# Two halves of a weight load either side of a clearing write: the opening of a mixture-of-experts kernel on one core

## The chip, the cores and the metric

The kernel runs on one core of a Trainium2 chip. The metric is the device time of one execution in microseconds (us), as the median of several runs. The core has five engines that run beside each other and wait for each other through semaphores: TensorE (PE: matmuls, with weight loads shown as PEld), VectorE (DVE), ScalarE (ACT), GpSimd (POOL) and SyncE (SP, which here only issues DMAs). Sixteen DMA engines serve all queues of the core: q1 is SyncE's, q10 ScalarE's, q0 GpSimd's (the indirect transfers).

## What is computed

The input x has 16 x 256 tokens of 128 numbers. Three layers follow each other, each on a layer-normed x: a mixture of experts, an attention without softmax over the keys, and the same mixture of experts again.

```python
x = x + 0.5 * ffn(layernorm(x), norm_scale, gate_w, gate_b, w1, b1, w2, b2)
x = x + attn(layernorm(x), Wq, bq, Wk, bk, Wv, bv, Wfq, bfq, Wfk, bfk)
x = x + 0.5 * ffn(layernorm(x), norm_scale, gate_w, gate_b, w1, b1, w2, b2)

# ffn, for T tokens, 32 experts, 4 chosen per token
t = rmsnorm(x) * norm_scale
vals, idx = top_k(t @ gate_w.T + gate_b, 4)
combine = zeros(T, 32) with softmax(vals) at idx
h1 = einsum('th,efh->tef', t, w1) + b1
glu, lin = min(h1[..., ::2], 7), clip(h1[..., 1::2], -7, 7)
h = glu * sigmoid(1.702 * glu) * (lin + 1) * combine[:, :, None]
out = x + einsum('tef,ehf->th', h, w2) + combine @ b2
```

Only the four chosen experts of a token have a weight, so the kernel computes these alone: it sorts the tokens by expert, and runs every expert on its own rows.

## The kernel before

**Tiling.** The 4096 tokens are two groups of four blocks of 512 tokens (four tiles of 128). The sorted rows of a group lie in DRAM in xs[g], and the experts' results in ys[g]; a row holds five tokens of one expert, and one expert step takes four times 25 rows (125 tokens each).

**Preparation (L129 to L270).** SyncE issues, in this order: small constants, the four x blocks of group 0 (L136), b1 (L138), w1 in four loads of 1024 KB, eight experts each (L244 to L246), the clearing of xs[0] in 14 writes of 500 KB from a zero tile (L252 to L255), w2 in four loads (L257 to L259), and zeros for the tail of ys (L266). The clearing is needed because experts read whole rows of xs and the sort fills only some of them; what it writes is overwritten where the sort has something to put. Group 1 has no such clearing: its dispatch is called with clear=True and scatters zeros to the free rows only.

**Folding w1.** `folded` (L293) multiplies a weight by the matrix `less`, which takes the mean over the input dimension off and scales by norm_scale; one TensorE product for two experts (two matmuls of 512 columns each in the trace), one ScalarE copy back into w_sb (L299). `fold_experts(c)` (L303) does experts 2c and 2c+1, so 16 folds cover w1; folds 0 to 3 need w1's first load, 4 to 7 the second, 8 to 11 the third, 12 to 15 the fourth. The PSUM tag "ph" that they write has two buffers.

**Routes and dispatch.** `routes` (L957) is a generator: norm coefficients of four blocks, then for each block the gate, the four best experts, their weights and ranks (`route`, L437 to L515), with a yield between pieces. `dispatch` (L519 to L668) is the sort of a group: its first piece counts rows per expert for the whole group (L524 to L570), the second makes the expert tables (pex, L577), and then for each of the four blocks one piece makes the row numbers (L628 to L645) and four pieces, one a tile, gather tokens with one-hot matmuls (p_f, L665), copy them to one of three buffers s (L669, L670) and scatter them to xs by an indirect DMA on GpSimd's queue (L589). So a group has 16 scatters. Each of them must follow the clearing of xs[0].

**Order of the work.** Generators wait in a queue; `step(n)` runs n pieces, `finish()` the rest. For group 0 the program appends routes(0), and writes 16 times step(2) and a fold; then the load of b1's rows into the last row of w_sb (L1015, which must follow all folds, since they read that row), finish, two constants (minus, mask), dispatch of group 0 and finish, `fold_attention` (L307), and the experts of group 0 with group 1's routes beside them. `experts` (L684) loads xq from xs on SyncE's queue (L696), copies the step's weights from w_sb on GpSimd (L703), transposes (L709), multiplies (L723, L741) and writes ys (L748). This written order isn't the order on the engines: the builder places each instruction on its engine's queue by its written place and by when it takes it to be ready, and each engine then runs its queue in that order.

Of the kernel before, what the change touches and what calls it, by code (L numbers as in the profile page):

```python
# [22 lines left out]
P = 128  # L23
# [5 lines left out]
NE = 32  # L29
# [27 lines left out]
def kernel(  # L57
# [22 lines left out]
    nc = tc.nc  # L80
# [160 lines left out]


    w_sb = wpool.tile([P, NE, EW], F32, tag="w_sb", name="w_sb")
    for c in range(NE // 8):  # L244
        s = slice(c * 8, (c + 1) * 8)
        nc.sync.dma_start(w_sb[:, s, 0 : 2 * P], w1[:, s].rearrange("h e t f -> h e (t f)"))  # L246
    FILLS = NT // NJ // 2
    part = NB * BW // P // (2 * FILLS)
    rows = xs[0][0:NB, :].rearrange("n w -> (n w)").rearrange(
# [2 lines left out]
    for i in range(FILLS):  # L252
        nc.sync.dma_start(
            rows[:, i],
            zero.rearrange("p r h -> p (r h)")[:, 0:part].unsqueeze(1).to_broadcast([P, 2, part]),  # L255
        )
    for c in range(NE // 8):  # L257
        s = slice(c * 8, (c + 1) * 8)
        nc.sync.dma_start(w_sb[:, s, 2 * P : EW], w2[:, s])  # L259
# [31 lines left out]
    LAST = P - 1  # L291

    def folded(w, name, out=None):  # L293

        pw = ps_h.tile([P, TB], F32, tag="ph", name=f"pw_{name}")[:, 0 : math.prod(w.shape[1:])]
        nc.tensor.matmul(pw, less, w, start=True, stop=True)
        if len(w.shape) > 2:
            pw = pw.rearrange("p (e c) -> p e c", e=w.shape[1])
        nc.scalar.copy((w if out is None else out)[0:LAST], pw[0:LAST])  # L299
# [3 lines left out]
    def fold_experts(c):  # L303

        folded(w_sb[:, 2 * c : 2 * c + 2, 0 : 2 * P], f"w{c}")
# [620 lines left out]
    def step(n=1):  # L926
        for _ in range(n):
            while waiting:
                try:
                    next(waiting[0])  # L930
                    break
                except StopIteration:
                    waiting.popleft()

    def finish():
        while waiting:
            step()
# [19 lines left out]
    def routes(g, gap, most):  # L957
        srcs = []
        for b in range(GB):
            if g > 0:  # L960
                load_x(g * GB + b)
            srcs.append(x_tiles.pop(g * GB + b))
        co = coefficients(srcs, f"f{g}")
        yield

        def block(b):
            yield from route(first[g], srcs[b], b, co[:, :, b * NJ : (b + 1) * NJ])

        yield from staggered((block(b) for b in range(GB)), gap, most)
# [38 lines left out]
    b1_rows = dram.tile([NE, 2 * P], F32, tag="b1_rows", name="b1_rows")  # L1008
    nc.scalar.dma_start(b1_rows, b1_t)

    waiting.append(routes(0, 1, GB))
    for c in range(NE // 2):
        step(2)
        fold_experts(c)
    nc.sync.dma_start(  # L1015
        w_sb[LAST:P, :, 0 : 2 * P], b1_rows.rearrange("(o e) c -> o e c", o=1)
    )
    finish()

    minus = const.tile([P, NJ, P], BF16, tag="minus", name="minus")  # L1020
# [16 lines left out]


    waiting.append(dispatch(first[0]))
    finish()  # L1040
    banks.clear()
    banks.append((ps_bg, "bg"))
# [72 lines left out]
```

## Time and profile before

| | us |
|---|---|
| median of 3 runs (lowest to highest) | 747.09 (746.89 to 747.17) |
| the profiled execution | 768.92 |
| its span | 767.2 |
| PE busy in the span | 646.2 (84%) |
| DVE, ACT, POOL busy | 489.8, 385.8, 291.2 |
| granted TensorE clock, mean | 0.922 |

The profile is one execution, recorded with the profiler on, and longer than the runs. A row of a timeline gives the start in us from the span's start, the duration, the engine and line, the operation with what it writes and reads, and in brackets how long the engine was idle before and what ended that (inferred from semaphores). Some rows of the opening, which the change touches:

```profile
7.71 6.38 SPq L246 DMA_DIRECT2D w_sb<-in_w_dram  x4
14.20 27.58 SPq L253 DMA_DIRECT2D xs<-zero  x14
42.78 6.76 SPq L259 DMA_DIRECT2D w_sb<-in_w_dram  x4
52.66 1.36 SPq L1015 DMA_DIRECT2D w_sb<-b_rows  x1
```

These are times of issue on SyncE's queue, not of landing; a group of issues is merged into a row with their number.

### The profile page before, as it was taken

To read this page: it belongs to the slowest core of one execution; us is meant where nothing else is said; L and a number is where in the kernel's file an instruction comes from. 1 tells how busy PE (TensorE), PEld (TensorE's weight loads), DVE (VectorE), ACT (ScalarE), POOL (GpSimd) and SP (SyncE) were. 2 spreads that over 40 slices of the span, in tenths; PEclk is the share of its full clock that TensorE was granted. 3 is DMA by queue.
4 is the path that set the end of the run, shared out by engine and by line. 5 is a ranking of instruction groups with operands and counts; after the bars stand their busy time and mean duration, and the time that the engine had idled before them with its cause. 6 is when DMAs were issued, how large, how long until landed. Compare 5 with 4: busy or idle time off the path is not lost. (4 is left out here: it accounts for less than half of the span.)

```text
span 767.2 us, 16355 instructions
## 1 busy us (share of the span) xinstructions
PE 646.2 (84%) x4995; PEld 602.6 (79%) x5009; DVE 489.8 (64%) x1833; ACT 385.8 (50%) x918; POOL 291.2 (38%) x583
## 2 busy tenths in 40 slices
PE   3877598879969998897987889888889769999776
PEld 1567588879868888896886889878878659999776
DVE  6864777755527988965763587678767436654534
ACT  2843498445517458465452547464665414545410
POOL 3024433676363432121464231321226265543152
PEclk9978799999979999997998988898989979999989
DMA  7997355665565635223446342522435466766464
GB/s 235 369 334 280 124 148 163 216 234 188 144 165 137 175 84 149 55 83 108 168 168 187 112 144 69 139 79 68 107 111 184 155 157 196 222 170 176 118 185 157
DMA packets 136924, 123.98 MB, mean 162 GB/s; under 512 B 9858, under 2 KB 123970, under 8 KB 136834
## 3 DMA queue, kind: packets, MB, share of 16 engines
q1 hardware_dynamic: 121890, 73.16, 33.8%
q0 software_dynamic: 10960, 44.90, 17.5%
q10 hardware_dynamic: 3984, 4.82, 1.8%
q8 instruction: 45, 0.74, 0.4%
q14 instruction: 45, 0.37, 0.1%
HBM read 58.80 MB, written 64.04 MB: 160 GB/s over the span
## 5 line engine op out<-in xcount | busy, mean ns | idle before, releaser
L703 POOL COPY w_l<-w_sb 128x256 f32 x192 | 72.5, 407 | 144.5 <-PE ph_l L723 124.4
L703 POOL COPY w_f<-w_sb 128x256 f32 x192 | 74.0, 417 | 121.7 <-PE ph_f L723 108.3
L723 PE MATMUL ph_f<-xT_f,w_f 128*128 128x125 f32 x768 | 104.7, 285 | 2.9 <-DVE lin_f L728 1.6
L723 PE MATMUL ph_l<-xT_l,w_l 128*128 128x125 f32 x768 | 102.5, 284 | 0.0
L723 PEld LDWEIGHTS ph_f<-xT_f,w_f 128*128 128x128 f32 x768 | 98.0, 201 | 4.8 <-POOL w_f L703 2.7
L723 PEld LDWEIGHTS ph_l<-xT_l,w_l 128*128 128x128 f32 x768 | 96.6, 200 | 1.0 <-issue 0.9
L728 DVE TENSOR_SCALAR lin_f<-ph_f 128x250 f32<-128x250 f32 x96 | 39.3, 413 | 56.5 <-ACT a_f L727 46.5
L728 DVE TENSOR_SCALAR lin_l<-ph_l 128x250 f32<-128x250 f32 x96 | 39.4, 413 | 56.1 <-ACT a_l L727 55.5
L665 PE MATMUL p_f<-tn_f,o_f 128*128 128x128 f32 x320 | 47.1, 310 | 14.6 <-ACT s_f L669 6.5
L665 PEld LDWEIGHTS p_f<-tn_f,o_f 128*128 128x128 f32 x320 | 44.3, 221 | 16.9 <-ACT s_f L669 7.2
L741 PE MATMUL po_l<-w_sb,a_l 128*125 x384 | 55.3, 288 | 2.5 <-DVE a_l L733 1.7
L741 PE MATMUL po_f<-w_sb,a_f 128*125 x384 | 53.9, 283 | 3.1 <-ACT yq_f L746 1.3
L741 PEld LDWEIGHTS po_l<-w_sb,a_l 128*125 128x125 f32 x384 | 49.8, 200 | 4.2 <-ACT yq_l L746 2.1
L727 ACT ACTIVATE a_f<-ph_f 128x250 f32<-128x250 f32 x96 | 36.3, 384 | 33.3 <-PE ph_f L723 23.2
L727 ACT ACTIVATE a_l<-ph_l 128x250 f32<-128x250 f32 x96 | 36.0, 380 | 33.7 <-PE ph_l L723 27.1
L814 PE MATMUL pu_f<-gt_f,u_f 128*128 128x128 f32 x320 | 48.5, 295 | 5.0 <-DMA gt_f<-ys,row_f 4.5
L814 PE MATMUL pu_l<-gt_l,u_l 128*128 128x128 f32 x320 | 44.0, 283 | 9.0 <-DMA gt_l<-ys,row_l 7.7
L741 PEld LDWEIGHTS po_f<-w_sb,a_f 128*125 128x125 f32 x384 | 47.9, 194 | 4.6 <-ACT yq_f L746 2.6
L814 PEld LDWEIGHTS pu_l<-gt_l,u_l 128*128 128x128 f32 x320 | 40.8, 197 | 12.1 <-issue 8.5
L784 POOL DMA_INDIRECT gt_f<-ys,row_f x32 | 32.3, 1010 | 47.1 <-PE pu_f L814 25.6
L814 PEld LDWEIGHTS pu_f<-gt_f,u_f 128*128 128x128 f32 x320 | 43.8, 208 | 6.2 <-DMA gt_f<-ys,row_f 3.5
L589 POOL DMA_INDIRECT xs<-s_f,row_f x32 | 31.1, 972 | 44.7 <-ACT s_f L670 21.6
(338 smaller groups left out, 1464.0 us busy)
## 6 DMA issues: line engine op xcount, KB each, us to landing
xq_f<-xs SPq DMA_DIRECT2D x48, 224.0 KB
ys<-yq_f SPq DMA_DIRECT2D x48, 224.0 KB
xq_l<-xs SPq DMA_DIRECT2D x48, 224.0 KB
ys<-yq_l SPq DMA_DIRECT2D x48, 224.0 KB
xs<-zero SPq DMA_DIRECT2D x14, 500.0 KB
w_sb<-in_w_dram SPq DMA_DIRECT2D x4, 1024.0 KB
x<-in_x_dram SPq DMA_DIRECT2D x8, 256.0 KB
xr_f<-xr_f ACTq DMA_DIRECT2D x8, 256.0 KB
```

The costliest lines, as they stand in the source:

```text
L589: ins = nc.gpsimd.indirect_dma_start(out=xs[st.g][:, :], out_offset=bass.IndirectOffsetOnAxis(ap=index, axis=0), in_=rows.rearrange("p r h ...
L665: nc.tensor.matmul(p0[:, r, :] if r < 4 else p1[:, 0:P], o[:, r, :], k.tn[:, t, :], start=True, stop=True,)
L703: nc.gpsimd.tensor_copy(w[:, s, :], w_flat[:, bass.ds(at[2 * c + s], 2 * P)])
L723: nc.tensor.matmul(ph[:, part, s, 0:RT], w_q[c][:, s, part * P : (part + 1) * P], x_q[:, 2 * c + s, :], start=True, stop=True,)
L727: nc.scalar.activation(a[:, ts, :], ph[:, 0, :, 0:RT], AF.Silu, scale=ALPHA)
L728: nc.vector.tensor_scalar(lin[:, ts, :], ph[:, 1, :, 0:RT], LIMIT + 1.0, 1.0 - LIMIT, ALU.min, ALU.max,)
L741: nc.tensor.matmul(po[:RT, t, :], hT[:, t, :], w_flat[:, bass.ds(at[t] + 2 * P, P)], start=True, stop=True,)
L784: nc.gpsimd.indirect_dma_start(out=gt.rearrange("p r h -> p (r h)"), out_offset=None, in_=ys[st.g][:, :], in_offset=bass.IndirectOffsetOnA ...
L814: nc.tensor.matmul(pu[:, t, :], u[:, r, s, :], got[t][:, r, :], start=(r == 0), stop=False)
```

## The change

The load of w1 becomes a function, and half of its loads (EARLY = 2 of four) stay ahead of the clearing of xs[0]; the other two go behind the clearing and ahead of w2. Folds 0 to 7 are written between three pieces of the routes each, and the routes are finished behind them. The constants minus and mask follow as before. Then the dispatch of group 0 is appended, and folds 8 to 15 are written after one piece of it each; b1's rows are loaded after fold 15, and the rest of the dispatch follows. No instruction is added or left out.

```diff
-    for c in range(NE // 8):
-        s = slice(c * 8, (c + 1) * 8)
-        nc.sync.dma_start(w_sb[:, s, 0 : 2 * P], w1[:, s].rearrange("h e t f -> h e (t f)"))
+    def load_w1(lo, hi):
+        for c in range(lo, hi):
+            s = slice(c * 8, (c + 1) * 8)
+            nc.sync.dma_start(w_sb[:, s, 0 : 2 * P], w1[:, s].rearrange("h e t f -> h e (t f)"))
+
+    EARLY = 2
+    load_w1(0, EARLY)
...
+    load_w1(EARLY, NE // 8)
     for c in range(NE // 8):
         s = slice(c * 8, (c + 1) * 8)
         nc.sync.dma_start(w_sb[:, s, 2 * P : EW], w2[:, s])
...
     waiting.append(routes(0, 1, GB))
-    for c in range(NE // 2):
-        step(2)
+    for c in range(4 * EARLY):
+        step(3)
         fold_experts(c)
-    nc.sync.dma_start(
-        w_sb[LAST:P, :, 0 : 2 * P], b1_rows.rearrange("(o e) c -> o e c", o=1)
-    )
     finish()
...
     waiting.append(dispatch(first[0]))
+    for c in range(4 * EARLY, NE // 2):
+        step()
+        fold_experts(c)
+    nc.sync.dma_start(
+        w_sb[LAST:P, :, 0 : 2 * P], b1_rows.rearrange("(o e) c -> o e c", o=1)
+    )
     finish()
```

## The prediction

> **What bounds the kernel now.** I read the page's slices first, then the stage that the change touches: the DMA queues by stretch, GpSimd's and ScalarE's timelines, and the waits of SyncE's queue. Of the page:
>
> ```profile
> PEclk9978799999979999997998988898989979999989
> DMA  7997355665565635223446342522435466766464
> ```
>
> Each column is 19.2 us. The DMA engines are full only in the first three columns; after that TensorE carries the time (busy 84% of the span). So the first 84 us are a stage of their own with another limit, and what ends it is in SyncE's waits of the first 150 us and in TensorE's row after it:
>
> ```profile
> SPq L696 <- DMA xs<-s_f,row_f: 25.1, 1, 25.1
> 87.19 1.06 PE L709 MATMUL pxT_f<-ident,xq_f 125*128 125x125 f32 x4 [7.91 <-DMA xq_f<-xs]
> ```
>
> The experts' first load waits for the last of the first group's 16 scatters, and TensorE has nothing before it lands. The time that counts is the issue of scatter 16; a shift of it moves the next 680 us with it. GpSimd's timeline of the 16 issues (cut):
>
> ```profile
> 49.68 1.15 POOL L589 DMA_INDIRECT xs<-s_f,row_f  x1 [14.71 <-DMA w_sb<-in_w_dram]
> 51.13 0.97 POOL L589 DMA_INDIRECT xs<-s_f,row_f  x1 [0.30 <-issue]
> 52.41 0.96 POOL L589 DMA_INDIRECT xs<-s_f,row_f  x1 [0.30 <-issue]
> 56.84 0.97 POOL L589 DMA_INDIRECT xs<-s_f,row_f  x1 [3.35 <-ACT s_f L670]
> ...
> 66.61 0.96 POOL L589 DMA_INDIRECT xs<-s_f,row_f  x1 [3.88 <-ACT s_f L670]
> ...
> 81.44 0.96 POOL L589 DMA_INDIRECT xs<-s_f,row_f  x1 [1.34 <-DVE st_f L344]
> ```
>
> Two paces: from issue 1 (49.68) to issue 7 (66.61) six intervals of 2.82 us; from there to issue 16 (81.44) nine of 1.65 us. Why the first is slow is in ScalarE's timeline and in the DMA queues, for 49.7 to 66 and then for 66 to 84 us:
>
> ```profile
> 46.79 0.27 ACT L670 COPY s_f<-p_f 128x128 f32<-128x128 f32 x1
> 55.81 0.59 ACT L669 COPY s_f<-p_f 128x512 f32<-128x512 f32 x1 [4.43 <-DMA xs<-s_f,row_f]
> ```
> ```profile
> DMA packets 4522, 5.77 MB, mean 354 GB/s; under 512 B 207, under 2 KB 4191, under 8 KB 4521
> q1 hardware_dynamic: 4121, 4.07, 80.6%
> q0 software_dynamic: 400, 1.69, 26.0%
> ```
> ```profile
> DMA packets 958, 3.65 MB, mean 203 GB/s; under 512 B 196, under 2 KB 262, under 8 KB 956
> q0 software_dynamic: 880, 3.55, 50.0%
> q1 hardware_dynamic: 76, 0.07, 1.1%
> ```
>
> s_f has three buffers, so the fourth copy waits until scatter 1, issued at 49.68, has landed at 55.81: 6.1 us, beside SyncE's backlog (q1: w2, ys zeros, group 1's x). After 66 us the backlog is gone and copies, TensorE and GpSimd set the pace. The first issue has another gate: its rows were ready at 46.79 + 0.27 = 47.06 us, GpSimd issued at 49.68. The row names w_sb, a load that a scatter doesn't need; of what it does need the DMA queue's last is the clearing of xs, 14 x 500 KB behind all of w1. I take the clearing as the gate (the releaser is inferred); q1's packets turn from 2 KB to 512 B (w2) between 45 and 47 us, which fits.
>
> **The change, part by part.**
>
> *The order on SyncE's queue.* Nothing is added or removed; two of the four 1024 KB loads of w1 (2.10 MB) go behind the clearing. From 16 to 44 us all queues together moved 10.30 MB (368 GB/s), 9.17 MB of it on q1, 328 GB/s. So the clearing ends between 2.10 / 0.368 = 5.7 and 2.10 / 0.328 = 6.4 us earlier; I take 5.8: the gate opens at 43.9. The late half of w1 lands where the clearing ended, its first piece at about 43 to 46 us. Moved behind it, w2, ys zeros, b1_rows and x of group 1 keep their place in bytes. b1_rows now waits for fold 15 in the sort and x of group 1 is queued behind it, but x landed near 66 us and its first user (bn_stats) runs at 77.5: some 10 us of cover, and without it about as much as the slip beyond.
>
> *Folds 8 to 15.* Eight times two matmuls (1.02 us a fold at full clock, 1.7 at half) and one ScalarE copy of 0.59 us leave the routes and go beside the first sort: 8.2 us of TensorE, 4.7 us of ScalarE. In the routes VectorE is busy 11.07 of 12.50 us (24 to 36.5), so they end at most 1 to 2 us sooner. From 36.5 to 44.2 ScalarE is busy 7.33 of 7.70; three fold copies (1.75 us) vanish from there. The first rows are then ready at about 47.06 - 1.5 - 1.75 = 43.8, level with the new gate. In the new place, 49.7 to 66, TensorE is busy 10.1 and ScalarE 3.5 of 16.3 us: the folds fit; I charge 0.3 us. Without that cover, or queued ahead of the sort, see the third rival.
>
> *step(3) and step(1), dispatch, minus and mask appended elsewhere.* Order only, no instruction more; mask and minus already run at 12.6 us. At nothing, plus or minus 1 us for a different order later on.
>
> *What an earlier first scatter is worth.* Not its 5.8 us, as the bytes are the same. Each scatter (5.24 MB / 16 = 0.328 MB) that moves before the backlog's end puts that end off by 0.328 / 0.354 = 0.93 us, and saves 1.65 us afterwards. With k more of them: k = (5.8 + 0.93 k) / 2.82, so k = 3.1; gain 3.1 x (1.65 - 0.93) = 2.2 us. Less 0.3 for the folds: **1.9 us**.
>
> [...] The row has 6.1 us for the first, 2.82 us between issues, and q0 26% of the engines. I go by the row.
>
> The profiled execution takes 768.92 us (span 767.2, 1.7 around it), the median of the runs 747.09; the 22 us between lie all over the execution. The shift is early and absolute, so it carries over one to one: 768.92 - 1.9 = 767.0 profiled, 747.1 - 1.9 = **745.2**. A measurement here tells about 0.2% (1.5 us) from no change.
>
> **The rivals.**
>
> *The start passes wholly (10%).* [...]
>
> *The start doesn't move (18%).* GpSimd's row names w_sb, and the rows were ready only at 47.06. If sort or another load sets issue 1, it stays within 1 to 2 us of 49.68 and k is below 1: 747.
>
> *Slower: TensorE stands at a fold (24%).* TensorE takes matmuls in order. Of the first sort, past's product, the row numbers and the first rows follow dispatch's first step, and folds 8, 9, 10 are written between these. If they are also issued so, the first rows stand behind w1's third piece, here about 45 us: then three folds at the half clock of that stretch (PEclk 0.50, 44.2 to 49.7), 5.1 us, ten matmuls of the first tile 2.1 us, copies and issue 1.0 us: issue 1 at 53.2, 3.5 us late. k = -3.5 / (2.82 - 0.93) = -1.9, x 0.72 = 1.3 us lost; the same wait for the fourth piece beside scatters adds 0 to 2, I take 0.6. 747.1 + 1.3 + 0.6 = 749. It decides when fold 8 stands ahead of the first tile's matmuls and its piece lands after 43 us. For it: order as written, and folds did wait for w_sb before (2.3 us in two waits). Against: in the profile instructions aren't in written order, fold_attention's matmuls (L315) run at 40.37 ahead of dispatch's L650, so the builder takes what it believes ready.
>
> **How the numbers follow.** Main case 48%, 743 to 746.8 (start 2 to 6 us earlier, order plus or minus 1). With the rivals: faster by over 0.2% (below 745.6): three quarters of the main case, all of the first, 46%; within: 12 + 15 + 4 = 31%; slower: 23%. Range 741.5 to 749.6, leaving out half of the first and half of the third case. Faster and slower together hold most; the likeliest case's own range is 743 to 746.8.
>
> **What would show it.** Right: issue 1 at 43.5 to 46 us; 2.5 to 3 us between issues until 67 to 69, then 1.65; issue 16 at 79 to 80; the first pxT some 2 us sooner. Packets on q1: 1 KB, 2 KB, 1 KB, 512 B. Rival 1: issue 16 near 75.6. Rival 2: issue 1 near 49 with the clearing landed at 44. Rival 3: a TensorE wait for w_sb of several us ahead of the first tile. Wrong altogether: issue 16 as I say, but the end elsewhere, since the experts' stage was put in another order.

## The result and the profile after

The changed kernel takes **746.61 us** (median of 21 runs, 736.37 to 753.45); the kernel before, run beside it, 748.51 us (21 runs, 743.15 to 753.22). The ratio of the medians is 0.9975, that of the means 746.72 / 748.44 = 0.9977: a gain of 1.7 to 1.9 us. The means have an error of 0.9 us (standard deviations 3.60 and 2.29, 21 runs each), so the sign is likely and the size is loose. The ratio that comes with an interval is 0.9946 [0.992, 0.9973]; it leaves out the slowest of the changed kernel's runs, those over 1.5% above a single run at 736.37, and so flatters it: I go by the medians of all.

The profiled execution takes 748.82 us, its span is 747.0, against 768.92 and 767.2 before. These 20 us are not the change, nor are they the profiler's: the control below was traced in 764.86 us, among its other runs (764.16 to 774.43). The unchanged kernel takes 769.76, 770.22 and 751.01 us on three chips, so I take the trace of before to be from a chip of the longer kind. From the first pxT on (the experts' first transposes), the trace of before needs 680.0 us to its end (87.2 to 767.2) and that of after 658.9 (88.1 to 747.0). From the point on where every instruction on VectorE has the same order in both, 158.8 and 151.3 us, it is still 608.4 against 595.7. Between the first pxT and that point the order is not the same, on any of the four engines that compute: there group 1's routes run beside the first experts, and the builder placed them otherwise. The second to fourth row of TensorE before, and the second of after:

```profile
88.92 1.09 PE L709 MATMUL pxT_f<-ident,xq_f 125*128 125x125 f32 x4 [0.67 <-ACT xT_f L711]
89.81 3.62 PE L723 MATMUL ph_f<-xT_f,w_f 128*128 128x125 f32 x16
93.22 1.01 PE L285 MATMUL pt_f<-ident,tn_f 128*128 128x128 f32 x4
```
```profile
88.94 1.06 PE L292 MATMUL pt_f<-ident,tn_f 128*128 128x128 f32 x4
```

Group 1's transposes (pt_f) have moved ahead of the experts' first products (ph_f). So the change reaches beyond the opening, and a gain could also lie there. Stages are best compared between traces of one chip. Of the page of after, the two rows that were shown of before:

```profile
PEclk9879899999979999897998998999979979999989
DMA  7999546787474534223455452522435577766464
```

A column is 18.7 us now. The picture is the same: DMA engines nearly full in the opening, about half used behind it. GpSimd's timeline of after, cut:

```profile
45.47 1.14 POOL L596 DMA_INDIRECT xs<-s_f,row_f  x1 [10.55 <-DMA w_sb<-in_w_dram]
...
49.92 0.96 POOL L596 DMA_INDIRECT xs<-s_f,row_f  x1 [1.37 <-ACT s_f L677]
...
55.77 0.96 POOL L596 DMA_INDIRECT xs<-s_f,row_f  x1 [0.94 <-ACT s_f L677]
60.78 0.96 POOL L596 DMA_INDIRECT xs<-s_f,row_f  x1 [4.04 <-ACT s_f L677]
...
65.67 0.96 POOL L596 DMA_INDIRECT xs<-s_f,row_f  x1 [2.66 <-ACT s_f L677]
...
78.65 1.75 POOL L710 COPY w_f<-w_sb 128x256 f32 x5
...
82.12 0.98 POOL L596 DMA_INDIRECT xs<-s_f,row_f  x1 [0.17 <-issue]
```

These are issues 1, 3, 4, 5, 7 and 16. Issue 1 is 4.2 us sooner than before (49.68), issue 3 still 2.5 us (52.41), issue 5 no longer (60.17 before), issue 7 0.9 us, issue 16 0.7 us later (81.44), behind copies of weights that before came after it. ScalarE and TensorE show who took the start's lead away:

```profile
44.90 0.27 ACT L677 COPY s_f<-p_f 128x128 f32<-128x128 f32 x1
54.74 0.59 ACT L676 COPY s_f<-p_f 128x512 f32<-128x512 f32 x1
```
```profile
48.74 5.48 PE L303 MATMUL pw_w<-w_sb,fold_b 128*128 128x512 f32 x12
54.05 0.61 PE L672 MATMUL p_f<-tn_f,o_f 128*128 128x128 f32 x4
...
88.08 1.07 PE L716 MATMUL pxT_f<-ident,xq_f 125*128 125x125 f32 x4 [9.01 <-DMA xq_f<-xs]
```

The first tile's rows are ready at 44.90 + 0.27 = 45.2 us and the first scatter follows 0.3 us later. But the fourth tile's last four matmuls stand behind twelve matmuls of folds, six folds in one piece, and ScalarE's copies of these folds stand ahead of the tile's own copy, which starts at 54.74. Before, that copy waited for scatter 1 to land and started at 55.81. Another wait has taken the place of the old one, at almost the same time.

The opening in the traces of this study, in us from the span's start. "Cleared" is the last packet of the clearing.

| kernel | cleared | rows 1 ready | issue 1 | issue 7 | issue 16 | first pxT |
|---|---|---|---|---|---|---|
| before | 47.4 | 47.1 | 49.7 | 66.6 | 81.4 | 87.2 |
| before, chip of batch 1 | 49.4 | 50.0 | 51.8 | 68.4 | 82.7 | 89.4 |
| before, cut A | 49.9 | 49.9 | 52.1 | 68.4 | 82.9 | 89.1 |
| before, cut B | 49.1 | 49.8 | 51.9 | 68.3 | 87.3 | 94.3 |
| after | 40.9 | 45.2 | 45.5 | 65.7 | 82.1 | 88.1 |
| after, cut A | 42.1 | 46.0 | 46.3 | 66.9 | 82.8 | 88.7 |
| after, cut B | 43.8 | 46.3 | 46.5 | 67.5 | 85.3 | 91.5 |
| loads only | 39.6 | 45.5 | 45.8 | 66.6 | 83.8 | 89.9 |
| mend | 42.3 | 46.7 | 47.0 | 66.8 | 82.6 | 89.7 |
| mend, cut A | 43.6 | 44.0 | 45.3 | 63.2 | 79.3 | 85.5 |
| mend, cut A, without ys zeros | 42.1 | 45.5 | 45.8 | 63.4 | 78.4 | 85.3 |
| spread, cut A | 41.7 | 43.9 | 44.2 | 60.4 | 80.7 | 92.0 |
| spread | 42.6 | 43.7 | 44.4 | 59.6 | 83.8 | 91.6 |
| steps only | 47.8 | 49.3 | 54.2 | 68.7 | 86.9 | 92.9 |

The start is told apart beyond doubt: every trace with the new loads issues at 44.2 to 47.0, every one with the old at 49.7 or later. The last columns are not: two traces of the unchanged opening differ by 5 us in the first pxT (89.1 and 94.3). On one chip (batch 1) the first pxT came no sooner with the new loads, 89.9 and 89.7 against 89.4. A gain of 2 us there can be read only from times over several runs.

### The profile page after: what moved, and what is told of

The parts are those of the page before. It is cut to its first block, busy times and chain, and to the rows that moved or that the text cites. A ratio compares the mean times of both kernels' runs of the same rounds, so it can differ in the third digit from the quotient of the medians.

```text
span 747.0 us, 16366 instructions
## 1 busy us (share of the span) xinstructions
PE 633.5 (85%) x5009; PEld 589.2 (79%) x5009; DVE 489.7 (66%) x1833; ACT 385.1 (52%) x918; POOL 291.9 (39%) x583
## 3 DMA queue, kind: packets, MB, share of 16 engines
q0 software_dynamic: 10960, 44.90, 18.1%
## 5 line engine op out<-in xcount | busy, mean ns | idle before, releaser
L730 PEld LDWEIGHTS ph_f<-xT_f,w_f 128*128 128x128 f32 x768 | 96.4, 198 | 4.4 <-issue 2.8
L735 DVE TENSOR_SCALAR lin_f<-ph_f 128x250 f32<-128x250 f32 x96 | 39.0, 412 | 49.8 <-ACT a_f L734 49.3
L748 PE MATMUL po_l<-w_sb,a_l 128*125 x384 | 54.2, 285 | 2.6 <-DVE a_l L740 1.7
L821 PE MATMUL pu_f<-gt_f,u_f 128*128 128x128 f32 x320 | 46.2, 285 | 3.8 <-DMA gt_f<-ys,row_f 3.3
L791 POOL DMA_INDIRECT gt_f<-ys,row_f x32 | 32.2, 1008 | 43.3 <-PE pu_f L821 16.2
L672 PE MATMUL p_f<-tn_f,o_f 128*128 128x128 f32 x320 | 42.2, 288 | 6.4 <-DVE o_f L664 4.3
L753 ACT COPY yq_l<-po_l 125x512 f32<-125x512 f32 x48 | 28.2, 588 | 36.6 <-PE po_l L748 31.9
L791 POOL DMA_INDIRECT gt_l<-ys,row_l x32 | 30.6, 956 | 41.7 <-PE pu_l L821 22.4
L672 PEld LDWEIGHTS p_f<-tn_f,o_f 128*128 128x128 f32 x320 | 39.6, 200 | 8.9 <-DVE o_f L664 4.0
```

The source lines that it names most:

```text
L672: nc.tensor.matmul(p0[:, r, :] if r < 4 else p1[:, 0:P], o[:, r, :], k.tn[:, t, :], start=True, stop=True,)
L730: nc.tensor.matmul(ph[:, part, s, 0:RT], w_q[c][:, s, part * P : (part + 1) * P], x_q[:, 2 * c + s, :], start=True, stop=True,)
L735: nc.vector.tensor_scalar(lin[:, ts, :], ph[:, 1, :, 0:RT], LIMIT + 1.0, 1.0 - LIMIT, ALU.min, ALU.max,)
L748: nc.tensor.matmul(po[:RT, t, :], hT[:, t, :], w_flat[:, bass.ds(at[t] + 2 * P, P)], start=True, stop=True,)
L753: nc.scalar.copy(yq, po[:RT])
L791: nc.gpsimd.indirect_dma_start(out=gt.rearrange("p r h -> p (r h)"), out_offset=None, in_=ys[st.g][:, :], in_offset=bass.IndirectOffsetOnA ...
```

## The experiments

My theory after the result (A): the gain is made in the opening, it is what the bytes behind the clearing let through, and nothing later takes from it. The rivals: the gain arises in the stage behind, from the other order (B in the expectations); there is none (C); the opening gains more and a later stage gives it back, or the folds on TensorE, or the six weight copies on GpSimd, hold back scatter 16.

**Batch 1, whole kernels on one chip.** They share 71 runs of the kernel before: median 769.76 us, mean 769.31.

*The kernel before, as a control.*

> The kernel before, unchanged, once more: a second trace of it, and the floor of what a ratio can tell. Theories for the change's gain: A (opening), the first scatter comes earlier and some of that reaches the first pxT; B (second stage), the first pxT comes no earlier, and the gain arises between 90 and 200 us, where group 1's routes run beside the first experts in another order on the engines; C, neither, the difference of the two traces is that of two executions. Every theory: ratio 1.000 within 0.003. Under B the stretch from the first pxT (87.2 us) to the 25th (217.1 us), 129.9 us in the first trace of before and 120.8 in that of the changed kernel, stays near 130; under C it falls near 121.

Measured: 768.63 us (22 runs, mean 768.91), ratio 0.9998 [0.9973, 1.0023]. So a comparison of this kind tells about 0.25%. The stretch from the first to the 25th pxT, 134.1 us here (89.4 to 223.5), is near the 130 that B asked for; but it was 131.9 and 130.5 in the traces of the loads alone and of mend on the same chip, so the 120.8 of the changed kernel is for the most part not the change's.

*The loads alone.* The new order of the loads, and the folds and the dispatch written as before:

```diff
+    load_w1(0, EARLY)
...
+    load_w1(EARLY, NE // 8)
```

> Only the loads are reordered (two loads of w1 behind the clearing); folds stay written beside the routes, two pieces each. A and B: the builder puts folds 8 to 15 behind the first four tiles of the sort by itself, as in the changed kernel, so issue 1 near 45.5 us, issue 15 and 16 behind weight copies on GpSimd (80.6 and 82.1), and the time of the changed kernel, about 2 us under before (ratio 0.995 to 1.000). The rival that the fold's place in the text matters: folds hold TensorE in the routes, issue 1 at 50 or later, ratio above 1.002.

Measured: 767.66 us (22 runs, mean 767.71), ratio 0.9961 [0.9935, 0.9988]. Of the means, 1.6 us sooner: as much as the whole change gained beside its own base (the changed kernel itself was not run in this batch). The trace shows why nothing is left for the other half: the builder set folds 8 to 15 behind the first three and a half tiles of the sort by itself, as in the changed kernel, since their part of w1 is queued behind the clearing, which ended at 39.6 us; the fourth tile's scatter was issued at 57.77. The written place of the folds did not decide where they went.

*The written order alone.* All of w1 ahead of the clearing, as before; the folds and the dispatch written as in the change:

```diff
-    for c in range(NE // 2):
-        step(2)
+    for c in range(4 * EARLY):
+        step(3)
         fold_experts(c)
...
+    for c in range(4 * EARLY, NE // 2):
+        step()
+        fold_experts(c)
```

> Only the writing order is changed (folds 8 to 15 after pieces of the first sort); all of w1 is loaded ahead of the clearing as before. A: the gate at issue 1 stays at 49 to 50 us, time as before (ratio 0.998 to 1.002). B: if the second stage's order comes from the writing order, the gain of the changed kernel (ratio about 0.997) is there without the loads.

Measured: 776.87 us (18 runs, mean 776.70), ratio 1.0089 [1.0063, 1.0115]: 7.4 us slower. Two rows of GpSimd's timeline, one right after the other:

```profile
53.06 0.11 POOL L443 MEMSET tn_f<- 128x4 f32 x1 [16.52 <-PE p_f L666]
54.24 1.15 POOL L590 DMA_INDIRECT xs<-s_f,row_f  x1 [1.07 <-DMA w_sb<-in_w_dram]
```

The rows were ready at 49.3 and the clearing's last packet ended at 47.8 us, so neither was what the scatter waited for until 53.06. A memset for group 1's routing (L443), which overwrites a tile that the sort still reads, stands ahead of the first scatter and waits for TensorE's products until 53.06. In the trace of before the same memset came behind issue 3. On TensorE, folds stand between the routes and the first rows too (from 39.88 on). What the last 1.1 us before 54.24 waited for, the trace doesn't tell. The memset is not the whole of the 7.4 us: against the control on this chip issue 1 is 2.5 us later, the first pxT 3.5, and the point where VectorE's order is the same again 6.2 (169.3 to 163.1); the stage behind the opening got another order too.

*Mend: the weight copies behind scatter 16.* The changed kernel, with the first eight copies w_f tied to follow the last scatter:

```diff
+                    with ExitStack() as behind:
+                        if name == "f0" and q < 2:
+                            behind.enter_context(tc.issue_after(scattered[name][-1].ins))
```

> The changed kernel, with the first eight weight copies of the first experts queued on GpSimd behind scatter 16 (order of issue only). In the changed kernel's trace six of these copies (2.15 us) stand ahead of scatters 15 and 16. A: issue 16 at 80.4 instead of 82.1, first pxT at 86.4 instead of 88.1, and 1.7 us less than the changed kernel: ratio to before 0.995. B: the first pxT moves as said but the total stays that of the changed kernel within 0.7 us, since the wait for group 1's scatters takes it up: ratio 0.9975.

Measured: 767.47 us (22 runs, mean 767.25), ratio 0.997 [0.9946, 0.9994]. The copies moved (w_f from 83.79, behind issue 16 at 82.65); against the loads alone the means differ by 0.5 us, with an error of 1.1. Issue 16 came at 82.65 and the first pxT at 89.7, where A had 80.4 and 86.4. The copies are not where a gain went, as far as this can tell.

**Batch 2, cut kernels on a second chip.** Cut A ends behind four steps of the experts of the first group, cut B behind two steps of the second group; what follows is left out and zeros are written as the result. The same cut is made in both kernels, in place of the loop over the experts' stages:

```diff
+    waiting.append(enter(1))
+    experts(first[0], 0, 4, lambda: step(3))
+    end = tmp.tile([P, NJ, P], F32, tag="xr", name="end", bufs=3)
+    nc.vector.memset(end, 0.0)
+    nc.vector.tensor_scalar(end[0:RT], tail[-1], 0.0, None, ALU.mult)
```

For cut B the second line is `experts(first[0], 0, NQS, lambda: step(3))`, then `finish()` and `experts(first[1], 0, 2, lambda: None)`.

> The kernel before, ended after four of the 24 steps of the first experts (everything later is left out, the output is zeros written at the end behind the last step): the opening by itself, free of the 650 us behind it. It serves as the base of cutA_after; about 87 us to the first pxT and 30 behind it, some 120 to 130 us.

> The changed kernel, cut in the same place. A (the gain is made in the opening): about 2 us less than cutA_before. B (it is made later) or C (no gain): the same as cutA_before within 0.7 us, since the first pxT came no sooner in the traces (89.9 and 89.7 against 89.4 us). In this cut one weight copy stands ahead of scatter 16 instead of six ahead of 15 and 16, so if these copies are what ate the gain, it shows here as 1.5 us more than in the whole kernel.

> The kernel before, ended after two steps of the second group's first experts (later work left out, zeros written at the end): opening and second stage, to about 220 us of the trace. Base of cutB_after; some 240 us.

> The changed kernel, cut in the same place. A: the difference to cutB_before is that of the cutA pair, 2 us. B: about 2 us here, and none in the cutA pair. C: none in either, within 0.7 us. The engines' order here is that of the whole kernel, six weight copies ahead of scatters 15 and 16.

Measured: cut A 126.01 us before (6 runs, mean 126.15) and 123.09 after (6 runs, mean 122.81), 2.9 us by the medians, 3.3 by the means with an error of 0.6. Cut B 234.72 (7 runs, mean 234.68) and 231.45 (5 runs, mean 231.13), 3.3 and 3.5 with an error of 1.1. Two of the seven runs of cut B before (230.9 and 232.1) are as short as those after (229.1 to 232.0), so cut B tells less than its error says. The whole gain is there when cut A ends, some 33 us behind the first pxT, and the next 108 us change it by less than the error. Cut A holds the opening and the first four steps, and these steps are in another order too. Traces of one chip show how open the share of each is:

| first pxT; same order again; between them (us) | before | after |
|---|---|---|
| first chip, control against the loads alone | 89.4; 163.1; 73.7 | 89.9; 159.6; 69.7 |
| first chip, control against mend | 89.4; 163.1; 73.7 | 89.7; 159.1; 69.3 |
| second chip, cut B | 94.3; 164.2; 69.8 | 91.5; 160.1; 68.6 |

"Same order again" is the point on VectorE named above. By then the new loads are 3.5 to 4.1 us ahead in each pair; but on the first chip all of it lies behind the first pxT, and in cut B 2.9 of 4.1 us lie ahead of it. These are single executions. So the gain is made before some 160 us, and by the times of cut A before some 122; that it is made in the opening alone, which is theory A, is not shown. No run kept the order behind the opening fixed. Whether some of it is lost in the 500 us behind cut B stays open: the whole kernel's 1.7 has an error of 0.9, and the difference between 3.3 and 1.7 is within both. The two traces of cut A, one execution each, differ by only 1.0 us in span (122.9 and 121.9) and 0.4 in the first pxT: read alone they would have hidden it (the one before is the shortest of its six runs, the one after the longest).

**Batch 3, the bytes against the folds, on a third chip.** The kernel before takes 751.01 us here (16 runs). The base is cut A of mend; two edits are made to it:

```diff
-    for g in range(n_grp):
-        rest = ys[g][NQS * NJ * BT :, :].rearrange("n w -> (n w)").rearrange(
...
```
```diff
-        step()
-        fold_experts(c)
+        while len(tiles) < c - 4 * EARLY + 5:
+            step()
+        with tc.issue_after(tiles[-1][0].ins), tc.issue_after(tiles[-1][1].ins):
+            fold_experts(c)
```

The first leaves out the 2.05 MB of zeros for ys, part of the backlog that the scatters run beside. The second ("spread") lets each of folds 8 to 15 follow the products and copies of one of the tiles 5 to 12.

> The changed kernel with the first eight weight copies behind scatter 16, cut after four expert steps (later work left out, zeros written at the end): base of the next two. Against cutA_after (123.1 us), where one copy stood ahead of scatter 16, at most 0.4 us less.

> As cutA_mend, without the zeros for the tail of ys (2 loads of 1000 KB left out, 2.05 MB of the backlog; the tail stays undefined). Byte theory: the backlog ends 2.05 / 0.354 = 5.8 us sooner, two scatters fewer fit beside it, so issue 16 and the end come 5.8 x (1 - 1.65 / 2.82) = 2.4 us sooner. Packet theory (scatters take their turn whatever else is queued) and fold theory: no more than 0.7 us.

> As cutA_mend, but folds 8 to 15 are queued one by one behind the products and copies of tiles 5 to 12 of the sort; in cutA_mend six of them stand between the products of the fourth tile. Fold theory: those six (5.5 us of TensorE, 5 us of ScalarE) are what held the fourth tile at issue 56 to 57 us; here it is issued at 52 to 53 and the cut ends 1.5 to 3 us sooner. Byte theory: the backlog on the DMA queues sets the pace anyhow; the fourth tile comes sooner, the later ones don't, and the end is within 0.7 us of cutA_mend.

Measured: the base 120.49 us (6 runs, mean 120.71); that is 2.6 less than the changed kernel's cut A, where at most 0.4 was expected, but on another chip, so it tells nothing of the copies. Without the zeros 117.97 (5 runs, mean 118.40): 2.5 us sooner by the medians, 2.3 by the means with an error of 0.9. The byte argument had put it at 2.4 and the others at no more than 0.7. So bytes are the likelier reading, on five and six runs. ScalarE's copies for the scatters of the base, and then without the zeros, show the same:

```profile
67.16 0.58 ACT L676 COPY s_f<-p_f 128x512 f32<-128x512 f32 x1 [4.24 <-DMA xs<-s_f,row_f]
...
70.20 0.58 ACT L676 COPY s_f<-p_f 128x512 f32<-128x512 f32 x1 [1.34 <-DMA xs<-s_f,row_f]
...
74.24 0.58 ACT L676 COPY s_f<-p_f 128x512 f32<-128x512 f32 x1 [1.02 <-DMA xs<-s_f,row_f]
```
```profile
63.86 0.58 ACT L667 COPY s_f<-p_f 128x512 f32<-128x512 f32 x1 [0.94 <-DMA xs<-s_f,row_f]
...
66.91 0.58 ACT L667 COPY s_f<-p_f 128x512 f32<-128x512 f32 x1 [2.30 <-PE p_f L663]
```

The brackets are to be read: between 56 and 80 us the copies of the base stood 9.3 us, in eight waits, for a scatter to land; without the zeros 2.8 us, in three, and from 65 us on TensorE is what they mostly wait for. These two traces moved less than the median did: issue 16 from 79.3 to 78.4, the first pxT from 85.5 to 85.3, the span from 118.5 to 118.1.

The spread cut took 125.25 us (6 runs, mean 125.06), **4.8 us more** than the base. The folds did get out of the way: issue 4 came at 51.8 instead of 54.7, issue 7 at 60.4 instead of 63.2, issue 12 still at 72.4 instead of 74.0. Then the fourth block of tiles began late, at 76.7 instead of 75.3, behind statistics of group 1 and a part of the attention's fold on VectorE, and issue 16 at 80.7 instead of 79.3. The end has another cause besides; TensorE of the spread cut, and of the base:

```profile
83.38 1.41 PE L292 MATMUL pt_f<-ident,tn_f 128*128 128x128 f32 x4 [3.35 <-DVE tn_f L451]
...
92.05 1.04 PE L722 MATMUL pxT_f<-ident,xq_f 125*128 125x125 f32 x4
```
```profile
85.48 1.07 PE L721 MATMUL pxT_f<-ident,xq_f 125*128 125x125 f32 x4 [7.56 <-DMA xq_f<-xs]
```

With the edit the builder set routing work of group 1 (pt, and behind it the gates) ahead of the experts' first transposes, and those came 6.6 us later. So the run doesn't tell cleanly what the folds cost at the end; it does show that a lead of 2.8 us at issue 7 (1.1 of it there at issue 1) was down to 1.6 at issue 12 and gone at issue 16.

*Spread in the whole kernel*, with both edits:

> The whole changed kernel with both mends: weight copies behind scatter 16, folds 8 to 15 one by one behind tiles 5 to 12. Fold theory: 1.5 to 3 us under the changed kernel, ratio to before 0.992 to 0.995. Byte theory: as the changed kernel and as mend, ratio 0.996 to 0.998.

Measured: 753.72 us (11 runs), ratio 1.0059 [1.0028, 1.009]: slower than before, where both theories had it faster. Issue 16 at 83.8, first pxT at 91.6. No version tried here is known to beat the changed kernel; it was not run in batches 1 and 3.

## Why the prediction was right, and where its working was not

**What bounds it: in part.** The first 84 us are a stage of their own, and cut A carries the gain. But the forecast's signs at the end of the opening didn't show: issue 16 came at 82.1, not at 79 to 80, and the first pxT at 88.1, not some 2 us before 87.2. Between traces of one chip the first pxT moved by 0.5 and 0.3 us later, and 0.4 (cut A) and 2.9 us sooner (cut B). And its last sign of being wrong, another order in the experts' stage, did come.

**The clearing as the first scatter's gate: held before, gone after.** With the old loads issue 1 comes 1.8 to 2.6 us after the rows and 2.2 to 2.8 after the clearing's last packet; with the new loads alone it follows the rows by 0.3 us, and so in every trace with them but two: cut A of mend and spread, where it comes 1.7 to 1.8 us after the clearing's last packet. So the second rival (the start doesn't move, w_sb named in the row) falls: the row still names w_sb, and the start moved 4.2 us, or 5.8 between the two traces of cut A (52.1 to 46.3). In no trace does issue 1 come less than 1.7 us after that packet, and with the old loads it doesn't follow the rows by 0.3 us: that speaks for the inferred gate. What fills the time from the last packet to the issue, 2.3 us in the trace of before (47.4 to 49.7), no trace shows.

**Clearing 5.8 us earlier: too small.** It measured 6.5 (47.4 to 40.9), and 7.8 in cut A. **Rows at 43.8, level with the gate: too early by 1.4.** They were ready at 45.2 and are the gate now. Issue 1 at 45.5 lies within the 43.5 to 46 of the forecast because both errors are small.

**Folds for 0.3 us, "they fit": this step failed.** The sum of idle time on TensorE was right and didn't matter: six folds stood as one block of 5.48 us ahead of the fourth tile's last matmuls, with the next block's row numbers behind them, and the 0.3 us charged for folds had no such queue in it. From 43.9 at 2.82 us an issue, the forecast has issue 7 at 60.8; it came at 65.7, a pace of 3.37. With the folds spread, the trace of the cut has it at 60.4, a pace of 2.70: about the pace forecast. From issue 1 to issue 7 that is 16.2 us against 17.9 with the block (the cuts of batch 3, one chip), so the block costs 1.7 us there; between the whole kernels, on different chips, 15.3 (spread) against 19.8 (mend). The third rival had the right engine and the right queueing, one place too early: it put folds ahead of the first tile's rows. That TensorE keeps the order of its queue shows in the trace of after: VectorE had written the four tiles (tn_f) for group 1's first transposes by 87.84 us, TensorE stood idle until pxT at 88.08, and the transposes followed it at 88.94. The 1.7 us for a fold at half clock was an estimate; the trace of steps only has 2.05 (at 39.88, granted clock 0.50).

**The byte argument, 3.1 scatters of 0.72 us: its price fits one test, its count isn't seen.** 2.05 MB less brought the end 2.3 to 2.5 us sooner, with an error of 0.9, where 2.4 was worked out from the same two paces; and a lead of 2.8 us at issue 7 was gone at issue 16 with the folds spread. But at 69 us the trace of after has eight issues and that of before eight too (the ninth at 69.50), not three more. The first rival, the whole start passing through, isn't seen: 4.2 to 5.8 us of start became 1.7 to 3.3 in the time. The low end of the range rests on it, and no run shows its term, scatters as fast beside the backlog as behind it (1.65 us an issue): from issue 1 to issue 7 the traces of the table have 2.4 to 3.5 us an issue.

**Order at nothing, plus or minus 1: too narrow.** The six weight copies ahead of scatters 15 and 16 cost nothing that could be measured (mend). But the other order behind the first pxT goes with a stretch that is 1.2 to 4.4 us shorter in the traces of one chip, which the forecast put at nothing without looking. And the same lines with the old loads cost 7.4 us, and a tie on eight folds 4.8.

So the total (1.9 forecast, 1.7 to 1.9 measured, 2.9 to 3.3 in the cut with an error of 0.6) is right, and so is its first half: the start moves by about what was said. That only a part of it is kept is right too; which part, and by what, is not settled. The folds cost more than was charged, the count of scatters isn't seen, and the order behind may have given a part of the gain. That these came out at 1.9 is in part luck.

## What to carry to other kernels

When a stage starts earlier beside a backlog on the same DMA engines, work out how much of the lead the bytes let through before counting it, and test it by taking bytes away. For work that is moved into idle time, ask which instruction it will stand in front of on each engine's queue, and in how large a block; the share of idle time doesn't answer that, and the written order doesn't either when a builder places the work. A gain of 2 us in 750 needs some twenty runs a side on one chip, or a cut that ends behind the stage, where it was 3 in 125. And before a gain is put down to one stage, compare the order of the instructions in the next: a builder may have changed it too.

## What the runs showed of the hardware

The same kernel took 748.5, 769.8, 770.2 and 751.0 us as medians of four sets of runs on one chip each: 2.9% apart, over ten times the effect under study. Within a chip single executions of a whole kernel scatter with a standard deviation of 2.2 to 3.8 us.

TensorE's granted clock in the trace of after, in rows that give a window in us, its length, TensorE's busy time (with the number of matmuls), the clock, and the DMA engines' share and rate:

```profile
32.00:36.00 4.00, 1.15 (x4) 0.61 1.06 362
36.00:42.00 6.00, 2.33 (x18) 0.50 0.73 211
48.00:52.00 4.00, 4.00 (x16) 1.00 1.17 336
```

The first tile's products run at the half clock: 2.12 us from their start to the copy (42.30 to 44.42, granted clock 0.50), against 1.23 for the fifth tile (58.52 to 59.75, granted clock 1.00). Before had the same (44.19 to 46.30, 2.11 us at 0.50), so it is no cost of the change, but by this difference 0.9 us of the path to the first scatter in both. The clock was full again from 46.6 us, after 4.3 us of TensorE without a gap (from 42.30); in the trace of before from 49.7, after 5.5 us (from 44.19). It had fallen at 32.9 us, when TensorE had been busy 1.58 of the last 4 us and no gap in them was longer than 1.4 us; in the trace of before at 39.4, after 2.65 busy us of 4. What sets it, these traces don't show, and whether the path gets shorter with TensorE kept busy there was not tried.
